# A product without use ahead of each row synthesis in the second layer's spectral mixers

## The chip, the cores and the metric

The kernel runs on one core of a Trainium2 chip. The metric is the device time of one launch in microseconds (us). Lower is better. The kernel before takes 3815.47 us, the median of three runs between 3814.44 and 3821.66.

## The reference, cut to what matters

The program is a network of four layers on an input of 4 x 32 x 128 x 128 float32 values. Layer 1 (counted from 0, so the second one) treats the 4 x 32 = 128 planes of 128 x 128 values as tokens, lets them attend to one another, and then sends each plane through two spectral mixers. Only the tail of that layer matters here:

```python
def spectral_conv(x, w, out_shape):
    wc = w[..., 0] + 1j * w[..., 1]                 # 32 x 17 modes are kept
    xft = jnp.fft.rfftn(x, axes=(-2, -1), norm='forward')
    top = jnp.einsum('bihw,iohw->bohw', xft[:, :, :mh, :mw], wc[:, :, :mh])
    bot = jnp.einsum('bihw,iohw->bohw', xft[:, :, -mh:, :mw], wc[:, :, mh:])
    ...
    return jnp.fft.irfftn(out_ft, s=out_shape, axes=(-2, -1), norm='forward')

def fno_layer(x, spec_w, skip_w, skip_b, out_shape, norm=None, act=None):
    xs = fourier_resample(conv1x1(x, skip_w, skip_b), out_shape)
    xf = spectral_conv(x, spec_w, out_shape)
    if norm is not None:
        xf = instance_norm(xf, *norm)
    y = xf + xs
    return act(y) if act is not None else y

# in codano_forward, after the attention:
    attn = fno_layer(attn, proj_w, proj_skip_w, proj_skip_b, (H, W))
    attn = instance_norm(attn + tokens, attn_norm_g, attn_norm_b)
    m = instance_norm(attn, norm2_g, norm2_b)
    m = fno_layer(m, mixer_w1, ..., (H, W), norm=(mixer_norm_g1, mixer_norm_b1), act=_gelu)
    m = fno_layer(m, mixer_w2, ..., (H, W), norm=(mixer_norm_g2, mixer_norm_b2))
    out = instance_norm(m, mixer_out_g, mixer_out_b) + attn
```

Three times per plane, an image of 128 x 128 values is made from 32 x 17 complex modes: for the projection, for the first mixer and for the second mixer.

## The kernel before, in words

The whole program is one TileContext on one core. `mixers` works on the 128 planes in 8 groups of 16 planes. For each group `group(g)` hands its steps to a planner, `Parts`: each step has an engine, an estimated cost, the steps it follows, and the buffers it takes and frees. The planner lists the steps by estimated start and rank, and `in_order` then pins this order on each of PE, DVE, ACT and POOL. A step that has to wait therefore holds back everything listed behind it on its engine. Groups overlap: while one group is normalized, others are transformed.

The inverse transform is `synthesize`, called three times per group under the names A (projection), B (first mixer) and C (second mixer), so 24 times in all. It has three kinds of steps:

- `columns` (line 1761, PE, twice): products of the modes with the table `sw` into the PSUM tile `pc`. They contract over 34 rows for A and over all 128 rows for B and C.
- `out` (line 1766, ACT, twice): the copy of `pc` to the SBUF tile `P1`.
- `rows` (line 1776, PE, once): the row synthesis. Eight products of 32 rows by 512 columns, from the tables `sh` and from `P1`, into the PSUM tile `pb`, which fills four banks. The four products of one `r` lie on four different strips of 32 rows of the PE array, and each writes a bank of its own.

There is one `pb` buffer (`plan.hold("pb", 1)`). A row synthesis can start when `P1` is copied and when the four DVE steps that read the previous `pb` are through. These readers are `addA` (line 1991), `addB` (line 2062) and `addC` (line 2094). Behind them follow the statistics (`bn_stats`, line 1918), small arithmetic on 16 x 1 columns, `spread` (line 1883, a product with ones), and the forward transform `analyze`: `along` (line 1798, products with the 64 columns of `fh`) and `freqs` (line 1815, products on half the columns of the array each). The scaled images go out through ACT (`affine`, line 1966) and POOL (`plus`, line 1973). `skip` (line 2053, DVE) makes the skip term, and `weigh` (line 1821, DVE) reads `freqs`' result.

All operands are float32. In the trace each float32 product stands as two matmul instructions, here called passes, each with its own weight load. A row synthesis is thus 16 passes.

Of the kernel before, what the change touches and what calls it, by code (L numbers as in the profile page):

```python
# [190 lines left out]
class Kernel:  # L191
# [1535 lines left out]
    def mixers(self, XG, Zl, mx, t1, t2, pt, pb, pc):  # L1727
# [5 lines left out]
        nc, ins, X, sc = self.nc, self.ins, self.X, self.sc  # L1733
# [8 lines left out]
        def add(kind, *args, **kwargs):  # L1742
            plan.rank = place[0] * 100.0 + self.MIX_RANKS[kind]
            return plan.add(*args, **kwargs)
# [5 lines left out]
        def synthesize(g, name, z, after, free, ready=()):  # L1750

            outs, c, hp = [], None, plan.hold("P1", 2)
            for q in range(2):
                h = plan.hold("pc", 2)

                def columns(q=q):
                    k = z().shape[0]
                    zv = z().rearrange("p (i j) k -> p i (j k)", j=4)
                    p = S[g][name, "pc", q] = pc.tile([P, 2, 2, P], F32, tag="pc", name="pc")
                    for i in range(2):  # L1760
                        nc.tensor.matmul(p[:, i], zv[:, 2 * q + i], self.sw[:k], start=True, stop=True)

                def out(q=q):
                    if q == 0:
                        S[g][name, "P1"] = t2.tile([P, 4, 2, P], F32, tag="P1", name="P1")
                    nc.scalar.copy(S[g][name, "P1"][:, 2 * q : 2 * q + 2], S[g].pop((name, "pc", q)))

                c = add("columns" + name, PE, 1.0, columns, [*after, c], take=[h] if q else [hp, h], free=free if q else [])
                outs.append(add("half" + name, ACT, 0.6, out, [c] + outs, free=[h]))

            def rows():
                p = S[g][name] = pb.tile([P, 4, 4, P], F32, tag="pb", name="pb")
                for r in range(2):
                    for j in range(4):
                        js = slice(32 * j, 32 * j + 32)
                        nc.tensor.matmul(
                            p[:, j], self.sh[js, j, r, :], S[g][name, "P1"][js, :, r, :], start=(r == 0), stop=(r == 1)
                        )

            h = plan.hold("pb", 1)  # L1780
            return add("rows" + name, PE, 2.0, rows, [*outs, *ready], take=[h], free=[hp]), h

        def every4(t, j):
# [1429 lines left out]
```

## Time and profile before

| | us |
|---|---|
| median of three runs (lowest, highest) | 3815.47 (3814.44, 3821.66) |
| the profiled execution | 3811.59 |
| span of its instructions | 3809.8 |
| first and last row synthesis start | 2530.4 and 2831.4 |
| mixers' stretch, 2527.8 to 2840.0 | 312.2 |
| PE, DVE, ACT, POOL busy in that stretch | 251.1, 244.2, 158.6, 119.0 |

The profile is of one execution. A page gives busy times by engine, the span in 40 slices, and the costliest groups of instructions. Further views give the same for a stretch of time (windows), the instructions in order (timeline), and who waited for whom (waits). PE is the matrix engine and PEld its weight loads. DVE, ACT and POOL are the vector, scalar and general engines. PEclk, and PEclk in the windows view, is the share of full speed that the chip granted the PE's clock. In the trace it is 1.0 or 0.5 at any moment, and it changes at multiples of 3.41 us.

### The profile page before, as it was taken

The numbers are of one execution on the slowest core, as the hardware profiler recorded it, in microseconds if no ns is written. First come the engines' busy times: TensorE is split into PE (matmuls) and PEld (weight loads), VectorE is DVE, ScalarE is ACT, GpSimd is POOL, SyncE is SP. The second block draws the span as 40 slices with busy tenths as digits, with TensorE's granted clock in tenths as the row PEclk, the third lists the DMA queues.
The fourth block names the chain that finished last, engine by engine and source line by source line (L and its number), as shares of the span: only waits on it lengthen the run. The fifth ranks groups of instructions, "written<-read, shape, count | busy, mean of one in ns | idle before, by whom it ended". The sixth has DMA issues, their size and how long they took to land. (4 is left out here: it accounts for less than half of the span.)

```text
span 3809.8 us, 64520 instructions
## 1 busy us (share of the span) xinstructions
PE 3133.8 (82%) x23495; PEld 2082.4 (55%) x23495; DVE 2938.7 (77%) x6986; ACT 2676.5 (70%) x5577; POOL 2525.0 (66%) x2043
## 2 busy tenths in 40 slices
PE   7888888888878888778888868787868987988877
PEld 4555455455545454455445447665547753587655
DVE  6788997898997898897789875577869856386942
ACT  5799896789896888886899873334566654176753
POOL 3699896699996799896799980133456522067940
PEclk8888899988999988899888885797869998998989
DMA  3000000000000000000000000000002000700003
GB/s 127 1 1 1 1 1 1 1 1 1 1 1 1 1 1 1 1 1 1 1 1 1 1 12 7 1 1 1 1 18 81 1 1 3 267 4 1 1 1 89
DMA packets 51654, 61.38 MB, mean 16 GB/s; under 512 B 5850, under 2 KB 31140, under 8 KB 51204
## 3 DMA queue, kind: packets, MB, share of 16 engines
q1 hardware_dynamic: 36740, 42.12, 3.3%
q10 hardware_dynamic: 14592, 15.08, 1.1%
q8 instruction: 188, 3.08, 0.3%
q14 instruction: 134, 1.10, 0.1%
HBM read 48.80 MB, written 8.39 MB: 15 GB/s over the span
## 5 line engine op out<-in xcount | busy, mean ns | idle before, releaser
L755 POOL TENSOR_TENSOR e<-dt,Ar 128x1024 f32<-128x1024 f32 x496 | 1180.1, 2412 | 33.4 <-ACT pa L761 32.2
L775 DVE TENSOR_TENSOR pa<-pa,S 128x1024 f32<-128x1024 f32 x496 | 607.0, 1224 | 49.6 <-ACT pa L761 48.7
L783 DVE SCALAR_TENSOR_TENSOR S<-u,BC,pa 128x256 f32<-128x256 f32 x1488 | 615.3, 475 | 22.8 <-DVE pa L775 1.4
L761 ACT ACTIVATE pa<-e 128x1024 f32<-128x1024 f32 x496 | 502.7, 1019 | 83.1 <-DVE S L783 37.6
L808 PE MATMUL yp<-S,Dp 64*64 64x256 f32 x4096 | 359.0, 504 | 122.3 <-issue 57.4
L808 PE MATMUL yp<-S,D 64*64 64x256 f32 x4096 | 293.9, 397 | 93.3 <-DVE S L795 69.7
L808 PEld LDWEIGHTS yp<-S,Dp 64*64 64x64 f32 x4096 | 192.8, 175 | 274.2 <-issue 155.9
L767 ACT ACTIVATE D<-I,BC 128x64 f32<-128x64 f32 x1024 | 262.5, 337 | 0.1
L808 PEld LDWEIGHTS yp<-S,D 64*64 64x64 f32 x4096 | 155.5, 138 | 185.4 <-issue 63.0
L1006 PE MATMUL pm<-h,Wm 128*128 128x512 f32 x512 | 237.0, 612 | 0.0
L826 PE MATMUL pm<-I,y 128*128 128x64 f32 x1024 | 171.9, 299 | 55.9 <-ACT y L816 55.9
L791 ACT ACTIVATE ub<-u,BC 128x256 f32<-128x256 f32 x496 | 210.1, 495 | 9.6 <-DVE S L795 6.8
L559 POOL TENSOR_TENSOR e<-e,den 128x512 f32<-128x512 f32 x128 | 131.7, 1041 | 118.6 <-DVE den L555 69.3
L772 POOL TENSOR_TENSOR Dp<-I,BC 128x256 f32<-128x256 f32 x256 | 156.2, 626 | 78.9 <-PE yp L808 70.5
L826 PEld LDWEIGHTS pm<-I,y 128*128 128x128 f32 x1024 | 162.1, 226 | 63.8 <-ACT y L816 63.8
L547 ACT ACTIVATE e<-sc,mn 128x128 f32<-128x128 f32 x512 | 145.9, 400 | 31.9 <-DVE mn L542 19.1
L1006 PEld LDWEIGHTS pm<-h,Wm 128*128 128x128 f32 x512 | 95.7, 194 | 116.4 <-issue 115.7
L795 DVE TENSOR_TENSOR S<-pa,ub 128x1024 f32<-128x1024 f32 x124 | 151.6, 1222 | 6.0
L821 PE MATMUL pm<-xc,DD 128*128 128x128 f32 x512 | 129.0, 338 | 5.3 <-DVE dt L1045 5.3
L542 DVE TENSOR_REDUCE mn<-sc 128x4 f32<-128x512 f32 x128 | 83.0, 680 | 57.3 <-PE sc L533 41.4
L821 PEld LDWEIGHTS pm<-xc,DD 128*128 128x128 f32 x512 | 88.8, 217 | 48.2 <-issue 37.1
L761 ACT ACT_TABLE_LOAD x88 | 112.9, 1283 | 1.5
(599 smaller groups left out, 8093.1 us busy)
## 6 DMA issues: line engine op xcount, KB each, us to landing
w<-in_L_ffn_weight_dram SPq DMA_DIRECT2D x22, 1024.0 KB, 14.7
w<-in_L_ffn_weight_dram ACTq DMA_DIRECT2D x10, 1024.0 KB, 13.7
out_dram<-o ACTq DMA_DIRECT2D x16, 256.0 KB, 2.9
out_dram<-o SPq DMA_DIRECT2D x16, 256.0 KB, 2.9
X<-in_x_dram SPq DMA_DIRECT2D x4, 512.0 KB, 5.6
A<-in_L_conv_A_log_dram SPq DMA_DIRECT2D x1, 2048.0 KB
cw<-in_L_conv_conv_w_dram SPq DMA_DIRECT2D x1, 512.0 KB
sh<-in_sh_dram SPq DMA_DIRECT2D x1, 512.0 KB, 3.7
```

The source lines that it names most:

```text
L755: nc.gpsimd.tensor_tensor(v["e", q], node("dt").unsqueeze(1).to_broadcast([P, 4, 256]), Ar[:, 4 * q : 4 * q + 4, :], ALU.mult)
L761: nc.scalar.activation(v["a", q], v.pop(("e", q)), AF.Exp, scale=-1.0)
L767: nc.scalar.activation(v["D", q][:, r, :], I2, AF.Copy, scale=g["BC"][:, i, s : s + 1])
L772: nc.gpsimd.tensor_tensor(v["D", q], I2.unsqueeze(1).to_broadcast([P, 4, 64]), C, ALU.mult)
L775: nc.vector.tensor_tensor(v["a", q], v["a", q], S[:, 4 * q : 4 * q + 4, :], ALU.mult)
L783: nc.vector.scalar_tensor_tensor(S[:, s, :], node("u"), Bt, a[:, r, :], ALU.mult, ALU.add)
L791: nc.scalar.activation(v["b", q][:, r, :], node("u"), AF.Copy, scale=g["BC"][:, i, s : s + 1])
L795: nc.vector.tensor_tensor(S4, v.pop(("a", q)), v.pop(("b", q)), ALU.add)
L808: nc.tensor.matmul(v["y"][o : o + 64, n, :256], D[ns, r, :], S[ns, s, :], start=(s < 2), stop=(s >= 14), skip_group_check=True,)
L821: nc.tensor.matmul(v["p"][:, j * P : (j + 1) * P], DD[:, j, :], g["xc"][:, j, cs], start=True, stop=False)
L826: nc.tensor.matmul(v["p"][:, o : o + 64], v["y"][:, n, j * P : (j + 1) * P], I2, start=False, stop=(n == 1))
L1006: nc.tensor.matmul(g["x", j], Wm[:, i, j * P : (j + 1) * P], rows(4 * k + 3 - i), start=(i == 0), stop=(i == 3))
```

## The change

Each row synthesis issues one more product, first of all. It multiplies the identity (128 x 128) with 256 columns of the table `sh` and writes into the first bank of `pb`. The first real product into that bank starts a new sum and overwrites it, so nothing reads the extra result.

```diff
             def rows():
                 p = S[g][name] = pb.tile([P, 4, 4, P], F32, tag="pb", name="pb")
+                nc.tensor.matmul(p[:, 0, :2, :], self.ident, self.sh[:, 0], start=True, stop=True)
                 for r in range(2):
                     for j in range(4):
                         js = slice(32 * j, 32 * j + 32)
                         nc.tensor.matmul(
                             p[:, j], self.sh[js, j, r, :], S[g][name, "P1"][js, :, r, :], start=(r == 0), stop=(r == 1)
                         )
```

The planner's cost for `rows` stays at 2.0, so the order of all other instructions stays the same on every engine: PE has 24 products more, the other engines have what they had. Lines behind 1772 move down by one. The wait for the free `pb` buffer moves from the first real product to the new one, and the wait for `P1`, where there is one, stays at the first real product.

## Prediction

> **What bounds the kernel now.** I first read the page's slices, to see what the PE and its clock do where the row syntheses lie, from 2530 to 2834 us: slices 27 to 30 of 40 (each 95 us).
>
> ```profile
> PE   7888888888878888778888868787868987988877
> DVE  6788997898997898897789875577869856386942
> PEclk8888899988999988899888885797869998998989
> ```
>
> PE and DVE are both mostly busy there, neither wholly, and the clock is below full. The windows view shows the mixers' stretch and, inside it, three places where the clock falls (columns: us; PE, PEld, DVE, ACT and POOL busy; granted clock; DMA).
>
> ```profile
> 2527.80:2840.00 312.20, 251.10 (x1432) 163.69 (x1430) 244.15 (x852) 158.60 (x337) 119.03 (x183) 0.79 0.00 1
> ...
> 2531.80:2535.20 3.40, 3.40 (x20) 2.08 (x12) 2.70 (x6) 1.17 (x2) 0.00 (x0) 1.00 0.00 0
> 2535.20:2538.60 3.40, 3.40 (x17) 1.22 (x16) 3.33 (x18) 0.59 (x1) 0.00 (x0) 0.50 0.00 0
> ...
> 2613.70:2617.10 3.40, 3.40 (x30) 3.22 (x30) 3.40 (x13) 0.77 (x2) 1.88 (x4) 1.00 0.00 0
> 2617.10:2637.60 20.50, 15.73 (x60) 8.43 (x60) 15.05 (x51) 8.68 (x21) 7.73 (x12) 0.50 0.00 1
> ...
> 2736.60:2740.00 3.40, 3.40 (x35) 3.22 (x30) 3.09 (x10) 3.40 (x10) 1.83 (x3) 1.00 0.00 0
> 2740.00:2746.80 6.80, 5.61 (x20) 4.82 (x20) 6.63 (x27) 4.44 (x11) 5.42 (x9) 0.50 0.00 0
> ```
>
> A mean clock of 0.79 means that 0.42 x 312 = some 130 us pass at half clock. Each of the three falls follows 3.4 us in which PE was busy throughout, so something other than busy time decides.
>
> Last come the timeline of PE and DVE's waits, for what one row synthesis costs and who needs it.
>
> ```profile
> 2634.69 3.42 PE L1776 MATMUL pb<-P,sh 32*128 32x512 f32 x16 [2.55 <-DVE t L2094]
> ...
> 2758.64 3.80 PE L1776 MATMUL pb<-P,sh 32*128 32x512 f32 x16 [1.98 <-DVE t L2062]
> ...
> 2805.15 2.00 PE L1776 MATMUL pb<-P,sh 32*128 32x512 f32 x16
> ...
> 2815.97 2.03 PE L1761 MATMUL pc<-sw,Zl 128*128 128x256 f32 x8
> ...
> 2826.98 3.78 PE L1761 MATMUL pc<-sw,Zl 128*128 128x256 f32 x8
> ...
> 2831.43 3.79 PE L1776 MATMUL pb<-P,sh 32*128 32x512 f32 x16 [0.68 <-ACT P L1766]
> ```
>
> ```profile
> DVE XG L1991 <- PE pb L1776: 12.2, 2, 11.7
> DVE t L2062 <- PE pb L1776: 9.3, 5, 4.1
> DVE t L2094 <- PE pb L1776: 5.2, 2, 4.0
> ```
>
> A row synthesis lasts 2.0 us at full clock and 3.8 at half; DVE directly waits for it only nine times. The page's chain of waits names no line of this stretch, so I followed the releasers back in the trace from the stretch's last scaled image (2849.7 us), by the page's rule. Of some 322 us, PE holds 190, DVE 107, ACT 21. 17 of the 24 row syntheses lie on this chain (those at 2592.9, 2625.3, 2715.8, 2734.8, 2749.2, 2775.4 and 2809.9 do not). So the stretch is bound by PE and DVE in turn, with no general slack on PE.
>
> **The change: what it adds.** Each of 24 products is two passes of 128x128 weights and 256 columns, the very shape of line 1761. Full clock: eight passes took 2.03 us, the last one's modelled length is 0.379, so a pass takes (2.03 - 0.38) / 7 = 0.236 us and the product 0.47. Half clock: (3.78 - 0.795) / 7 = 0.426, the product 0.85. Before, 15 row syntheses start at full clock and 9 at half, so PE gets 15 x 0.47 + 9 x 0.85 = 14.7 us more work.
>
> **What of it lies on the path.** The product takes over the wait for `pb`, so where PE sat idle for DVE (2.55 us at 2634.7, 1.98 at 2758.6) it cannot use the idle time: it starts when the real products would have. Where PE came straight from other work it pushes them back. Only a wait for `P1` hides it, since that wait stays with the real products; the chain has one with PE idle, at 2831.4, and its 0.68 us cover all but 0.17. Of the 17 on the chain 10 start at full clock, 4.7 us; 6 at half, 5.1; and that last one, 0.17. Sum 10.0 us. Every link of the chain is a semaphore or an engine's own order, and both stay, so without a change of clock the end moves by at least this. The seven off the chain I take at nothing: their readers are busy with other steps when they finish (after the one at 2625.3 the next reader starts 2.6 us late). With that cover gone they add 5 x 0.47 + 2 x 0.85 = 4.1, so the upper bound is 14.1. No engine loses or gains an instruction otherwise; nothing is queued past a new wait, since it is the old wait one product earlier; no DMA is touched.
>
> **What the clock gives back.** For each 3.41 us between possible clock changes I added up what the matmuls stream, in full-array columns: passes x columns x share of the 128 rows in use, with products side by side on array columns counted once. In this stretch the sum divides the cases without exception: wherever the clock stayed or became full it was 1609 or more, wherever it stayed or became half 1512 or less. Row synthesis is dense by this measure, 16 x 512 / 4 = 2048 columns in 2 us; the new product is 2 x 256 = 512, a third of the bound. So it can hold the clock up, but only in a window that falls short by less than that. The twelve falls had 1450, 1374, 1370, 1082, 1026, 1018 and then 884 or less. The three best are those shown above, and near row syntheses. The one at 2535.2, if avoided, runs the row synthesis there in 2.0 instead of 3.7 us: 1.7 back. The one at 2617.1 is followed by line 1761's 16 passes in 7.6 us, all on the chain; at full clock 3.9: 3.7 back. The one at 2740.0 would only come a window later, for PE is mostly waiting for ACT there: 0. At half clock the new product extends a burst that already runs at the array's full rate; of nine such bursts seven already raise the clock. So 5.4 us are within reach, and both depend on where a window's edge lies. Against that, four windows kept full clock with 1613 to 1690 columns, and a delay of their content can lose one, at about 1.7 us each. I take 2 us back net: +10.0 - 2 = +8. Bounds: 0 to all of the chain's PE time at half clock, 72.2 us, halved: 36.1.
>
> [...]
>
> **Profiled execution and median.** The sum is made in an execution of 3811.59 us (span 3809.8, 1.8 outside it), 3.9 below the median of 3815.47. I add to both: 3819.6 for such an execution, 3823.5 for the median. About 0.2%, 7.6 us, is what a measurement of this kernel can tell from no change.
>
> **Rivals.** (1) The forecast: the products cost their place on the path and the clock falls about as often; +7.6 to +14.1. Chance 0.56. (2) The clock gives back more than 2.4 us but less than 17.6: with both reachable falls avoided +10.0 - 5.4 = +4.6, 3820.1; this also holds the case that the product hides in some slack. For it: three falls within 240 columns of the bound. Against it: a moved edge takes as easily as it gives. Chance 0.28. (3) Faster: the added columns keep the array loaded enough that falls merge or vanish, and PE's 72.2 us at half clock on the chain shrink by half or more. It decides from 10.0 + 7.6 = 17.6 us of the 36.1; with 20 back it is 3805.5. For it: 24 times 512 columns is a third of the bound in a quarter of the 91 windows, and each avoided fall shifts all later windows. Against it: nine of twelve falls end windows short by over 400 columns, most without a row synthesis, and the product never fills idle time before one. Chance 0.16. (4) That the product isn't issued is excluded: it stands in PE's order 24 times.
>
> **Numbers.** Likeliest 3823.5, its own range 3823 to 3830. The range goes from 3808, where the third case begins (leaving its 0.16 out), to 3830, the upper bound 3815.5 + 14.1. Faster 0.16, same 0.28, slower 0.56.
>
> **What would show it.** 24 groups of two passes on line 1773, 0.47 or 0.85 us before each line 1777; those after a wait for DVE starting at its release. The stretch from 2527.8 longer by about 8 us, with a clock near 0.79. A clock of 0.85 or more there speaks for the third case; a stretch of the same length with the clock as before would mean that the chain had slack and the 10.0 is wrong; a growth outside the stretch would mean that something else acts.

## The result, and the profile after

| | before | after |
|---|---|---|
| median, us (lowest to highest; 8 runs each) | 3816.65 (3814.44 to 3821.66) | 3830.54 (3827.25 to 3833.62) |
| the profiled execution, us | 3811.59 | 3830.04 |
| start of the first columns product | 2527.50 | 2530.39 |
| from there to POOL's last addition into `X` | 328.73 | 338.00 |
| from there to the end of the span | 953.6 | 959.9 |

The change makes the kernel 13.9 us slower: a ratio of 1.0036, 95% interval 1.0026 to 1.0047. The direction is the forecast one. The size was forecast at +8 and at most +14.1, so the difference of 13.9 lies just inside; the median itself lies 0.5 us above the upper end of 3830, which was reckoned from the 3815.47 of three runs, where eight runs now give 3816.65. From here on "stretch" means the third line of numbers, from the first columns product to POOL's last addition (line 1973 before, 1974 after), and "rest" the last line.

The page's slices (each 96 us) show little: in slices 27 to 30 PE reads 8885 tenths, where before it read 8786.

```profile
PE   7888878888778888778888869788858987998877
DVE  6798987898997898897789865677769756386942
PEclk9888889988899988899888875797879998999999
```

The windows view shows more. The columns are us, then busy time of PE, PEld, DVE, ACT and POOL, then the granted clock. Kernel before, the stretch, the rest, and a part of the rest:

```profile
2527.50:2856.23 328.73, 253.08 (x1440) 165.24 (x1440) 251.42 (x881) 171.12 (x369) 131.24 (x203) 0.78 0.02 5
2856.23:3809.80 953.57, 803.52 (x5170) 595.54 (x5170) 613.28 (x2135) 526.41 (x1307) 431.52 (x427) 0.94 0.13 45
3175.16:3410.95 235.79, 204.79 (x2051) 143.61 (x2052) 138.70 (x483) 92.91 (x201) 71.64 (x81) 0.95 0.30 111
```

After, the same three, then the three places where the prediction saw a fall within reach:

```profile
2530.39:2868.39 338.00, 264.28 (x1488) 169.88 (x1488) 252.82 (x881) 170.93 (x369) 131.15 (x203) 0.79 0.02 4
2868.39:3828.20 959.81, 807.27 (x5170) 599.74 (x5170) 614.62 (x2135) 526.41 (x1307) 430.37 (x427) 0.94 0.13 45
3187.73:3427.94 240.21, 211.63 (x2052) 147.25 (x2053) 138.23 (x483) 93.23 (x201) 71.51 (x81) 0.91 0.29 109
...
2534.70:2538.10 3.40, 3.40 (x22) 2.01 (x15) 2.08 (x4) 0.72 (x2) 0.00 (x0) 1.00 0.00 0
2613.20:2616.60 3.40, 3.40 (x32) 3.33 (x30) 3.17 (x15) 2.99 (x4) 0.54 (x1) 1.00 0.01 2
2616.60:2620.00 3.40, 3.40 (x28) 3.24 (x29) 3.02 (x15) 1.17 (x2) 0.33 (x1) 1.00 0.00 0
2620.10:2643.80 23.70, 20.07 (x73) 11.88 (x76) 16.95 (x56) 8.87 (x21) 9.17 (x15) 0.50 0.00 1
2749.70:2753.10 3.40, 2.48 (x23) 2.30 (x22) 2.81 (x11) 3.40 (x11) 2.56 (x5) 1.00 0.00 0
2753.20:2759.90 6.70, 6.12 (x18) 4.06 (x20) 6.11 (x24) 3.83 (x9) 3.13 (x5) 0.50 0.00 0
```

PE has its 48 passes more (1440, 1488) and nothing else has changed in number. The stretch grew by 9.27 us. The rest, where the two programs have the same instructions (5170 passes in both), grew by 6.3 us, 4.4 of it in the one part shown, where the clock fell from 0.95 to 0.91. A further 2.9 us passed before the stretch, where nothing differs either; the experiments whose start was left alone begin their stretch anywhere from 2525.8 to 2533.7, so that is scatter. The sum, 18.5, is the difference of the two profiled executions. The medians differ by less, 13.9, because both profiles of the kernel before (3811.6, and 3810.2 in r7) are 5 to 7 us faster than its median; their stretches begin early, at 2527.5 and 2525.8.

The timeline of PE shows the new groups:

```profile
2533.32 0.70 PE L1773 MATMUL pb<-sh,ident 128*128 128x256 f32 x2
2533.95 2.00 PE L1777 MATMUL pb<-P,sh 32*128 32x512 f32 x16
...
2538.74 0.70 PE L1773 MATMUL pb<-sh,ident 128*128 128x256 f32 x2
2539.37 2.00 PE L1777 MATMUL pb<-P,sh 32*128 32x512 f32 x16
...
2640.36 1.19 PE L1773 MATMUL pb<-sh,ident 128*128 128x256 f32 x2 [2.56 <-DVE t L2095]
2641.49 3.18 PE L1777 MATMUL pb<-P,sh 32*128 32x512 f32 x16
...
2770.20 1.19 PE L1773 MATMUL pb<-sh,ident 128*128 128x256 f32 x2 [1.01 <-DVE t L2063]
2771.32 3.12 PE L1777 MATMUL pb<-P,sh 32*128 32x512 f32 x16
```

In these groups 0.63 us at full clock and 1.13 at half pass from the start of a product to the start of its row synthesis, not 0.47 and 0.85. The second group did run at full clock, in 2.0 us, where before it took 3.7. And the two groups behind a wait for DVE begin at DVE's release, as was said.

DVE's waits for `pb`, in the stretch:

```profile
DVE XG L1992 <- PE pb L1777: 13.2, 3, 12.3
DVE t L2063 <- PE pb L1777: 12.9, 5, 4.6
...
DVE t L2095 <- PE pb L1777: 5.0, 3, 2.5
```

DVE waits directly for a row synthesis 11 times, 31.1 us, against 9 times and 26.7 us before: a growth of 4.4 us. The other half of the 9.3 us does not stand in these waits.

### The profile page after: what moved, and what is told of

It is laid out like the page before. It is cut to its first block, busy times and chain, and to the rows that moved or that the text cites. A ratio compares the mean times of both kernels' runs of the same rounds, so it can differ in the third digit from the quotient of the medians.

```text
span 3828.2 us, 64612 instructions
## 1 busy us (share of the span) xinstructions
PE 3149.5 (82%) x23543; PEld 2091.4 (55%) x23543; DVE 2940.2 (77%) x6986; ACT 2675.9 (70%) x5577; POOL 2530.6 (66%) x2043
## 6 DMA issues: line engine op xcount, KB each, us to landing
w<-in_L_ffn_weight_dram ACTq DMA_DIRECT2D x10, 1024.0 KB, 14.1
```

## The experiments

The stretch is read from each run's profile. Its numbers, with the us at half clock in it, the rest, and the median over that of the kernel before in the same comparison:

| run | stretch | half clock | rest | median, us over before |
|---|---|---|---|---|
| before / after | 328.73 / 338.00 | 146.9 / 139.1 | 953.6 / 959.9 | +13.9 |
| r1 the changed kernel again | 337.98 | 139.1 | 961.9 | +15.3 |
| r2 product over 34 rows | 342.30 | 157.1 | 954.8 | +16.2 |
| r3 product of one column | 341.38 | 152.8 | 958.9 | +17.7 |
| r4 product of 512 columns | 351.23 | 142.1 | 956.4 | +23.5 |
| r5 before, start 1.2 us later | 330.99 | 140.2 | 954.5 | +9.0 |
| r6 before, start 2.4 us later | 339.96 | 170.8 | 955.2 | +12.6 |
| r7 before again | 328.72 | 146.9 | 953.8 | -7.2 (one execution) |
| r8 before, products in idle time | 322.38 | 113.4 | 957.3 | -2.1 |
| r9 after, additions of zero | 338.45 | 143.0 | 958.4 | +12.8 |
| r10 before, additions of zero | 325.25 | 143.5 | 954.3 | -4.5 |
| r11 after, start 2.4 us later | 342.38 | 149.4 | 961.9 | +20.8 |
| r12 before, wide `along` | 320.95 | 108.4 | 961.2 | -3.2 |
| r13 after, four repeats | 338.00 | 139.1 | 958.2 | +12.4 |
| r14 before, nine repeats | 328.66 | 146.9 | 955.3 | +3.9 |
| r15 before, diagonals by scalar | 331.71 | 136.4 | 953.9 | +2.6 |
| r16 r15 and the products | 335.95 | 126.9 | 957.2 | +9.3 |
| r17 after, two repeats | 338.00 | 139.2 | 959.3 | +9.3 |
| r18 r12, two repeats | 320.85 | 108.4 | 954.7 | -7.9 |

### r1 to r4: the product again, and of other sizes

r1 is the changed kernel. The others change the one line:

```diff
 r2
-nc.tensor.matmul(p[:, 0, :2, :], self.ident, self.sh[:, 0], start=True, stop=True)
+nc.tensor.matmul(p[:, 0, :2, :], self.ident[:34], self.sh[:34, 0], start=True, stop=True)
 r3
+nc.tensor.matmul(p[:, 0, 0, :1], self.ident, self.sh[:, 0, 0, :1], start=True, stop=True)
 r4
+nc.tensor.matmul(p[:, 0], self.ident, self.sh[:, :2], start=True, stop=True)
```

> The changed kernel once more, for a second trace of it. Theory A (the products lengthen the path by their own 14.9 us on the chain, and the columns that they add to the array keep the clock up somewhat more often, about 5 us back, so the mixers' stretch is 9 to 10 us longer): the stretch is again 9 to 10 us longer than the 312 before, the kernel 13 to 15 us slower in all, and the 4 to 5 us outside the stretch come from clock changes that fall differently in each execution, so their place in the trace changes. Rival X (the added instructions shift something in the later layers): the later layers are longer by the same 4 to 6 us at the same places as in the first trace.

> The product contracts over 34 rows instead of 128, with the same two passes of 256 columns: the same time on PE, a quarter of the load on the array. Theory A: the 4 to 5 us that the clock gives back are mostly lost, so the kernel is 17 to 19 us slower than before, and the clock in the mixers' stretch falls back from 0.81 to about 0.78. Rival B (the load of the product has no effect, only its time on the path counts): the same 14 us slower as the full product, within 2 us.

> The product has one column instead of 256: the wait, the weight loads and the number of instructions stay, the streaming and the load go. Theory A: about 0.2 us per product from its weight loads and the change of shape, 17 of 24 on the path: 2 to 5 us slower than before. Rival X (the number of added instructions shifts something in the later layers by 4 to 6 us): 7 to 10 us slower, with the surplus outside the mixers' stretch.

> The product has 512 columns: 0.43 us more at full clock and 0.85 more at half, and twice the load. Theory A: the path takes some 17 x 0.55 = 9 us more than with 256 columns, and the clock gives back some 4 us more: 18 to 20 us slower than before, clock in the stretch 0.84 or more. Rival B (load has no effect): 14 + 9 = 23 us or more.

The changed stretch repeats to 0.02 us. The table sets the growth of the stretch beside the products' own time (the sum over all 24, from a product's start to that of its row synthesis):

| | products' own time, us | stretch over before, us |
|---|---|---|
| after, r1 | 18.6 | 9.3 |
| r2 | 18.9 | 13.6 |
| r3 | 9.2 | 12.7 |
| r4 | 32.1 | 22.5 |

With 34 rows of 128 in the product (r2), products that took as long cost 4.3 us more, and 18 us more passed at half clock. The traces show where this begins. For 236 us r2's clock changes where that of the changed kernel does, to 0.05 us. Then comes the product that the last two timeline lines of the changed kernel show, at 2770.20. In r2 it reads:

```profile
2773.61 1.19 PE L1773 MATMUL pb<-sh,ident 34*128 34x256 f32 x2 [1.02 <-DVE t L2063]
2774.74 3.80 PE L1777 MATMUL pb<-P,sh 32*128 32x512 f32 x16
```

Counted as in the prediction, the step of 3.41 us that holds it has 1783 full-array columns in the changed kernel, and the clock rises behind it; in r2 it has 1318, and the clock stays at half for another 20 us. So at this place the columns of the full product brought the clock up. The medians alone would not tell: r2's +16.2 and r1's +15.3 agree within their intervals.

A product of a single column (r3), 2 full-array columns instead of 512, cost more than its own time (12.7 us, against 9.2) and more than the whole product (9.3) at twice its length. It was expected to cost 2 to 5 us. r4 was expected 18 to 20 us slower at a clock of 0.84; it came out 23.5 slower at 0.80, which is the total that rival B, without an effect of load, had named. So the price is no sum of lengths. Moving the work against the clock's pattern cost time too, 2.3 and 11.2 us in the next runs, and with the columns of the full product less time passed at half clock than with r3's single one, 139.1 us against 152.8.

### r5, r6 and r7: no product, another start

```diff
 r5: n = 2; r6: n = 4
+if q == 7:
+    for _ in range(n):
+        nc.scalar.copy(Zl[:34, :, 28:32], p[:34].rearrange("p k t -> p t k"))
```

The repeated copy, with the same result, stands just ahead of the stretch. r7 is the kernel before.

> The kernel before, without any product added; the last copy into Zl is repeated twice on ACT, so that the mixers' stretch starts about 1.1 us later and is otherwise the same. In all five traces so far a possible clock change lies 0.86 to 0.90 us behind the stretch's first product. Theory C (the place of the work against these edges decides how much of the stretch runs at half clock, and any shift redistributes it): the stretch itself gets longer or shorter by 2 us or more, beside the 1.1. Rival D (the stretch has a length of its own, and the products cost what they take on the path): 1 us slower, the stretch within 1 us of its 312.

> As the one before with four repeated copies, so that the stretch starts about 2.3 us later against the clock's edges. Theory C: the stretch's length changes by 2 us or more, and by another amount than with two copies; if the kernel before sits at a lucky place, both are longer, by up to 10 us. Rival D: 2 us slower, the stretch within 1 us of its 312.

> The kernel before once more, for a second trace of it. Its first profiled execution was 5 us faster than its median. If the stretch is again 312 to 313 us long and the rest is longer, the 4 to 6 us that the changed kernel lost behind the stretch are not the change's; if the layers behind the stretch are as fast as in the first trace, they are.

In the runs whose start was not moved, the next possible clock change comes 0.80 to 0.90 us behind the stretch's first product, and the pattern behind it repeats: r7 shows every clock change of the stretch where the kernel before has it. Moving the start by 1.2 us (r5) lengthens the stretch by 2.3 us, and moving it by 2.4 us (r6) by 11.2, more than all 24 products do. What r6 loses is seen in the windows view: PE begins with twelve passes on 34 rows, the clock falls, and it stays at half for 27.3 us in which PE is busy without a break. The copies do two things at once, however: they move the start, and they lengthen PE's wait ahead of it from 0.67 to 1.89 (r5) and 3.11 us (r6), so that less work lies ahead of the first possible change (550 full-array columns in the step of 3.41 us that holds r6's start, 1735 before). These runs do not separate the two. r5's median is 9.0 us over that of the kernel before, its profiled execution, the fastest of its ten, only 2.6; what the others did has no trace.

```profile
2537.90:2565.20 27.30, 27.30 (x97) 16.80 (x96) 10.23 (x37) 4.68 (x8) 0.00 (x0) 0.50 0.00 0
```

### r8: the same product where PE is idle

The product of the change, 43 times, each in a wait of PE for DVE (`FILL` lists the steps), and none ahead of a row synthesis:

```diff
+def fill(step, p):
+    i = seen[step] = seen.get(step, -1) + 1
+    for _ in range(self.FILL.get((step, i), 0)):
+        nc.tensor.matmul(p[:, :256], self.ident, self.sh[:, 0], start=True, stop=True)
```

> The kernel before, with none of the 24 products; instead 43 such products of 128 rows and 256 columns are put where PE waited longest for DVE in the trace of before (ahead of 11 steps of total, product, mean and var, into the PSUM tile that the step has taken already and overwrites), from 2 to 8 each, sized to the idle time. Theory A and C (the load on the array decides the clock, and the chain holds 72 us of PE work at half clock): the clock in the mixers' stretch rises from 0.79 to 0.88 or more, and the stretch gets shorter by 5 to 15 us. Rival D: the products hide in idle time at best, the stretch is as long as before or longer by up to 5 us.

```profile
2530.25:2852.63 322.38, 269.27 (x1524) 179.00 (x1524) 252.66 (x881) 170.69 (x369) 131.19 (x203) 0.82 0.02 5
```

16 us more of PE work than in the kernel before, and the stretch is 6.4 us shorter: 33.5 us fewer pass at half clock, though the clock reached 0.82 and not the 0.88 expected. So here the columns added in waits won time. The whole is hardly faster (0.9995, interval 0.9986 to 1.0004), for the rest is 3.8 us longer.

### r9, r10 and r11: the end and the start moved

```diff
 r9 (after, 3 images, once), r10 (before, 4 images, twice)
+zero = t1.tile([P, 4, P], F32, tag="zero", name="zero")
+nc.gpsimd.memset(zero, 0.0)
 self.mixers(XG, Zl, mx, t1, t2, pt, pb, pc)
+nc.gpsimd.tensor_tensor(self.X[:, :4, :], self.X[:, :4, :], zero[:, :4, :], ALU.add)
 r11: the four copies of r6, in the changed kernel
```

> The changed kernel, with one more step on POOL between the mixers and the next layer: it adds zeros to three planes of X (about 1.0 us), and the next layer's first statistics wait for it. Theory C2 (the layers behind the mixers take 953.6 to 955 us where the next possible clock change lies 2.4 us behind their beginning, as in both traces of the kernel before, and 959 to 962 us where it lies at 0, as in both traces of the changed kernel; 1.0 us of delay moves the one to the other): the layers behind shrink to 954 to 956 us, and the kernel is 4 to 5 us faster than the changed kernel in spite of the added step, 8 to 10 us slower than before. Rival X (the layers behind are slower for another reason): 1 us slower than the changed kernel, 14 to 16 us slower than before.

> The kernel before, with two such steps of four planes each (about 2.5 us) between the mixers and the next layer, so that the layers behind begin where those of the changed kernel did against the clock's edges. Theory C2: the layers behind take 959 to 962 us instead of 953.6, so 7 to 10 us slower than before with the mixers untouched. Rival X: 2.5 us slower.

> The changed kernel with the start of the mixers' stretch delayed by four repeated copies, at which the kernel before lost 11 us in the stretch (340.0 instead of 328.7, counted from its first product to its last addition into X). Theory C (the product's effect depends on where the work lies against the clock's edges; the 9.3 us at the first place are partly the loss of a good place): at this place, which is bad already, the products cost little, the stretch takes 335 to 345 us, less than 5 above the same place without products. Rival D (the products add what they take on the path, wherever the stretch starts): 349 us.

r9 and r10 missed their purpose, because the additions did not run at the end: POOL's order took them up at 2661.6 and 2657.3, in the middle of the stretch. There they did something else, and r10 became faster (0.9988, interval 0.9979 to 0.9997). The timelines of DVE and POOL show how. Before:

```profile
2650.30 5.48 POOL L1973 TENSOR_TENSOR X<-X,t 128x256 f32<-128x256 f32 x8
2650.33 5.53 DVE L1875 TENSOR_TENSOR dg<-n,ident 16x64 f32<-16x64 f32 x1
...
2655.91 0.69 PE L1883 MATMUL pt<-dg,ones 16*128 16x64 f32 x2 [7.29 <-DVE dg L1875]
```

r10:

```profile
2655.79 1.39 POOL L1977 TENSOR_TENSOR X<-X,t 128x256 f32<-128x256 f32 x2
2655.82 1.44 DVE L1879 TENSOR_TENSOR dg<-n,ident 16x64 f32<-16x64 f32 x1
...
2657.26 1.26 POOL L1175 TENSOR_TENSOR X<-X,zero 128x512 f32<-128x512 f32 x1
```

A DVE step on 16 x 64 values took 5.5 us while POOL ran eight additions in a row, and PE waited 7.3 us for it. In r10 the first addition of zero left POOL idle for 0.08 us behind two of them, and the same step was through after 1.4 us. The stretch is 3.5 us shorter and the pattern of the clock behind that point is the old one, one step of 3.41 us earlier. In r11 the later start costs the changed stretch 4.4 us, where it cost the kernel before 11.2: with the products in it, the first half clock ends after 6.8 us (another 3.4 follow soon), not after 27.3.

### r12: longer products elsewhere

Each product of `along` streams two copies of its 64 columns and writes them into two slots of `pc`, of which the next product overwrites the second:

```diff
-nc.tensor.matmul(p[:, i], m()[:, 8 * q + i, :], self.fh, start=True, stop=True)
+n = min(2, 8 - i)
+nc.tensor.matmul(
+    p[:, i : i + n], m()[:, 8 * q + i, :], self.fh.unsqueeze(1).to_broadcast([P, n, 64]),
+    start=True, stop=True,
+)
```

> The kernel before, without the 24 products; the products of the forward transform (along) stream 128 columns instead of 64, seven of each eight: the table fh twice, the second half falling into the next image's place in pc, which the next product overwrites. A pass of these takes 112 ns at full clock, as long as its weight load, so the columns should cost no time; the load on the array by this step doubles. Theory A and C (load decides the clock): the clock in the stretch rises from 0.78 to 0.85 or more, the stretch shortens from 328.7 to 310 to 323 us. Rival D: the passes take longer or nothing changes: 328 to 335 us.

The timeline of PE in r12, where the row ahead of the change reads `128x64 f32 x32` at the same 3.79 us:

```profile
2551.04 3.79 PE L1799 MATMUL pc<-fh,XG 128*128 128x128 f32 x32
```

A pass of 128 columns took as long here as one of 64, 0.12 us (3.79 us for 32 of either), so these columns cost no time and only raised the sum of columns. For 89 us the clock changes as in the kernel before; then the step that held 1375 full-array columns there holds 2524, and the fall that came at 2617.1 is put off by 10 us. The stretch lost 7.8 us and 38.5 us at half clock. But the rest took 961.2, and the median gained 3.2 us only.

### r13, r14, r17 and r18: the rest

In the profiles up to r12 the rest took 953.6 to 961.9 us over the same instructions. It went with the place of the stretch's end between two possible clock changes. Where the next one came 3.18 to 3.31 us behind the end, the rest was 953.6 to 955.2 (before, r2, r5, r6, r7, r10); where it came 0.77 to 0.84 us behind, 958.9 to 961.9 (after, r1, r3, r11, r12); r4, r8 and r9 lie at other places and between these, at 956.4 to 958.4. (r15, 0.18 us behind, has 953.9 and r16, 2.77 behind, 957.2.) These runs move that place, by repeats in the next layer's first normalization step:

```diff
 n = 4 (r13, after), 9 (r14, before), 2 (r17, after), 2 (r18, r12)
-for i in range(4):
+for i in [0] * n * (u == 0) + [0, 1, 2, 3]:
     nc.vector.tensor_scalar(x[:, i, :], xs(u)[:, i, :], mv[:, i, 0:1], rs[:, i : i + 1], ALU.subtract, ALU.mult)
```

> The changed kernel, in which the next layer's first normalization (DVE) repeats its first step four times, some 1.0 us on the path, with the same result. If the place of the stretch's end between two possible clock changes sets the time behind it, the distance from the 4901st DVE instruction to the next possible change goes from 3.41 to about 2.4 us, as in the kernel before, and the time behind the stretch, the repeats included, falls from 959.9 to 954.5 to 956: a ratio to the kernel before of about 1.0025. If the products spoil something else there, it becomes 961, with a ratio of 1.0039. The stretch itself stays at 338.0.

> The kernel before with nine such repeats, some 2.3 us, no product. If the place between two possible clock changes sets the time behind the stretch, the distance goes from 2.43 to about 0.1 us, as after the change, and the time behind, the repeats included, goes from 953.6 to 961 to 962: a ratio of about 1.0020. If not, it becomes 956, with a ratio of 1.0006. The stretch stays at 328.7.

> The changed kernel with two repeats of the first step of the next layer's normalization, 0.38 us each by r13. The end of the stretch lies 0.82 us ahead of a possible clock change; 0.77 us of delay puts the work behind it where the kernel before has it, to 0.2 us. If that place sets the time behind the stretch, it falls from 959.9 to 954 to 955.5, the repeats included, the profiled time to 3823 to 3826 and the median to 1.0020 of the kernel before. If not, it becomes 960.6, with 1.0039.

> r12 with the same two repeats: its end lies 0.78 us ahead of a possible clock change too, and the time behind it was 961.2. If the place sets that time, it falls to 954 to 955.5; the stretch stays at 320.9, and the whole is 6 to 7 us faster than the kernel before in the profiles, a ratio of about 0.9975. If not, 962 and a ratio of 0.9991.

A repeat cost 0.38 us. So r13 moved the work behind it by 1.54 us, past the place that was aimed at; its rest still fell from 959.9 to 958.2, which is 3.3 us won back against its delay but the fall of 1.7 misses the 954.5 to 956 expected and is no more than the 2.0 us between after and r1, two executions of one kernel. r14 moved it by 3.45 us, one whole step, and so kept its place; its rest grew by 1.7, less than the delay. r18 did what was expected:

```profile
2533.14:2853.99 320.85, 236.85 (x1440) 153.89 (x1440) 251.60 (x881) 170.95 (x369) 131.13 (x203) 0.83 0.02 4
2853.99:3808.70 954.71, 799.76 (x5170) 594.12 (x5170) 616.42 (x2137) 525.79 (x1307) 430.98 (x427) 0.95 0.13 45
```

With 0.77 us of added work its rest fell by 6.4 us. r18 is faster than both kernels: a ratio of 0.9980 to the kernel before, interval 0.9971 to 0.9989 (r12: 0.9980 to 0.9998). r17 was the same edit on the changed kernel and missed in its profile: 959.3, with the place set as in r18 to 0.05 us. Its median came down to +9.3, but with an interval of 1.0017 to 1.0041 that overlaps that of the change. So r18 speaks for the place, r13 weakly, and r17 shows that the place alone does not decide it. A rival stays open: that the products themselves do something to the work behind. None of the nine runs with all 24 products on 128 rows has a rest under 956.4, and of those without only r12 (961.2) and r8 (957.3) have one over 955.3. Against it stand r12, slow behind the stretch without a product, and r2, whose products on 34 rows leave 954.8.

### r15 and r16: the products on another stretch

```diff
-nc.vector.tensor_tensor(
-    d[:, :n, :], S[g]["n"][:, i : i + n].unsqueeze(2).to_broadcast([16, n, 16]),
-    self.ident[:16, :16].unsqueeze(1).to_broadcast([16, n, 16]), ALU.mult,
-)
+for j in range(n):
+    nc.vector.tensor_scalar(
+        d[:, j, :], self.ident[:16, :16], S[g]["n"][:, i + j : i + j + 1], None, ALU.mult
+    )
```

> The kernel before, in which DVE makes each diagonal ahead of a spread by one product of the identity with a scalar for each 16 columns, in place of one product of two tiles. If only the product of two tiles waits for a gap between POOL's additions (5.5 us in one place, 4.2 in another), each such step takes 0.2 us or less, PE's 7.3 us of idle time before one row synthesis shrink to some 2, and the stretch falls from 328.7 to 320 to 325; a ratio near 0.9980. If the scalar form waits as well, the stretch stays at 328.7 or grows by 1 to 2 us for the additional instructions.

> The same edit on the changed kernel: the 24 products on top of r15. If the products' price is their place on the path, at 0.6 us at full and 1.0 at half clock, with the clock's part set by where the stretch happens to lie, the stretch is longer than r15's by another amount than 9.3 us, between 4 and 14. If 9.3 is a fixed price of the change, it is 9.3 again, to within 0.5.

The scalar form was held up in the same way: four steps took 5.99 us beside the eight additions, where a single one took 0.22 us shortly before and after them.

```profile
2655.36 5.99 DVE L1876 TENSOR_SCALAR dg<-ident,n 16x16 f32<-16x16 f32 x4
...
2655.43 5.47 POOL L1973 TENSOR_TENSOR X<-X,t 128x256 f32<-128x256 f32 x8
```

Yet r15 gave another stretch with another pattern, 331.7 us, and on it the same 24 products cost 4.2 us instead of 9.3. The 9.3 is thus no fixed price of the change.

## Why the prediction was right and wrong

**Right.** The products are issued 24 times and lie on the path; those behind a wait for DVE start at its release. The stretch grew by 9.3 us where +8 was forecast, at a clock of 0.79. The first near fall, at 2535.2, was avoided: that window now holds 1938 full-array columns instead of 1370, and the row synthesis there is 1.7 us shorter. At the second the clock was kept for one window (1814 columns) and fell in the next (1424), with nothing won; the third won nothing either. The seven off the chain were nearly right: of them two have joined the chain followed in the changed kernel, which holds 19 products.

**Mis-sized, in the first term.** "A pass takes 0.236 us and the product 0.47" was read inside a run of eight equal passes. Next to another shape the next pass started later in the changed kernel. At full clock it is mostly 0.32 us from the product's first pass to its second (0.22 behind a pass of line 1761 with the same shape), and 0.31 from there to the row synthesis. The 24 took 18.6 us (16 at full clock, 9.8; 8 at half, 8.8), not 14.7. The 17 on the chain, forecast at 10.0, would be 12.7 by that factor; on the chain after stand 14.9 us.

**Mis-sized the other way, in the second term.** Of these 14.9 us, 5.6 do not show in the stretch, where 2 were forecast. PE work other than the products lies at half clock on the chain for 64.1 us instead of 72.2, which is 4 us of time given back by the clock. The other 1.6 us cannot be put down to one cause, for the chain takes other steps (ACT holds 12.9 us of it instead of 20.8). The errors of the two terms nearly cancel by luck, so the +8 of the stretch came out close to the measured value with two wrong terms. It could have come out otherwise: the same edit cost 4.2 us on r15, a smaller one 12.7 (r3), a later start without any product 11.2 (r6).

**The step that failed: "I add to both".** The sum was carried from the profiled execution to the median with nothing for the time behind the stretch. The prediction named growth outside as a sign "that something else acts", and it came: 6.3 us in the profile (8.3 in r1). The instructions there are the same; the longer stretch moved its end by 9.27 us, which is 2.7 steps of 3.41 us, and the work behind met the clock's steps at another place. That this place can cost or win as much is what r18 shows by moving the end alone, 6.4 us, on r12; on the changed kernel r13 won back 3.3 us against its own delay and r17 1.4. So why the rest grew stays open in part, and so does how much of the 6.3 us is in every execution: the medians differ by 13.9, which leaves 4.6 outside the stretch, and an unprofiled execution has no trace. That the forecast's upper bound of +14.1 still holds this sum is luck too: it was reckoned from the seven row syntheses off the chain, not for the work behind the stretch.

**The rivals.** The second had the clock's gain right (2.4 to 17.6 us; it was 4 to 5.6), but its sum, below +7.6, missed the 9.3, for it used the same cost of 10.0. The third, that columns make falls merge or vanish, names something real, but elsewhere: in waits (r8) and in passes that took 0.12 us with 64 columns and with 128 (r12), 33.5 and 38.5 us of half clock vanished. Ahead of dense row syntheses, 7.8 did, which fits its counter-argument, "the product never fills idle time before one".

**The columns that divided the windows.** In the trace of the changed kernel every window of the stretch with 1664 or more full-array columns was followed by full clock and every one with 1591 or less by half. Over twelve of these kernels, every window above 1591 was followed by full clock and every one below 1489 by half. The forecast's bounds, 1512 and 1609, were a little too sure: windows of 1591 stayed at half, and windows of 1489 kept full clock. The sum is my own reckoning from the matmuls in the traces; what the clock itself goes by was not shown.

## What to carry to other kernels

The price read inside a run of equal passes, 0.47 us for a product, was too low where the product stood between two other shapes, mostly 0.63 us, so take it from a change of shape in the trace. Where the clock of these traces moved in steps of 3.41 us, a small shift cost or won far more than its own length (2.4 us cost 11.2 in r6, and the work behind took 953.6 to 961.9): give such an edit a range from a run that shifts the work without the edit, not only from its own length. Columns that added no time to the stretch, in waits (r8) or in passes of the same length (r12), came with 33.5 and 38.5 us less at half clock, and the end of the stretch had then to be set as well (r18, 6.4 us).

## What was not expected of the hardware

- Being busy did not bring the clock back: PE was busy in 27.30 of 27.30 us in r6 and stayed at half clock, with 544 to 1539 full-array columns in each window before the last.
- One DVE step took 5.53 us beside eight additions of POOL in a row, which took 5.48, and 1.44 us in r10, where POOL was idle for 0.08 us behind two of them. The DVE steps of the stretch that were over 0.5 us longer than the shortest of their line add up to 21.4 us before (11 of them) and 22.2 after (12), so they are hardly a part of what the change cost.
- A pass of 128 x 128 weights took 0.12 us with 64 columns (before) and with 128 (r12).
